# Four convolution layers on one core: norm rows of the first two channels by TensorE, and another order of loads and late stores between layers 0 and 1 and between 2 and 3

## The chip, the cores and the metric

One core of a Trainium2 chip. The metric is the device time of one execution in microseconds (us), lower is better; the kernel before and the kernel after are each run several times and medians are compared. A core has five engines, each with its own instruction stream that it works through in order: TensorE (PE, with its weight loads as PEld), VectorE (DVE), ScalarE (ACT), GpSimd (POOL), and SyncE (SP), which in this kernel does no arithmetic and issues all the DMA transfers. An engine whose next instruction has to wait holds up everything queued behind it.

## What is computed

The input x is 32 images of 96 channels of 56 by 56, float32. Four residual layers follow one another, each on a group norm without weights (32 groups of 3 channels):

```python
x = x + L0(gn(x))   # 1x1 expand to 576, 3x3 depthwise, squeeze-excite, 1x1 project, + its input
x = x + L1(gn(x))   # 5x5 depthwise plus a 3-level Haar wavelet of 5x5 depthwise filters
x = x + L2(gn(x))   # the expand/depthwise/project block with 4-bit weights and activations
x = x + L3(gn(x))   # 9x9 depthwise, kernel made from a 2x2 matrix per channel
```

The norm needs, for each image and group, a mean and a variance over all its 56 x 56 x 3 values. So no part of an image can be normalized until all of that image is there.

## The kernel before: how it works

**Layers 0 and 2** go image by image with channels on partitions; the order of their steps on TensorE, VectorE and ScalarE is written by hand as a string per image (`L0_ORDER`, `L2_ORDER`, `MANUAL`). **Layers 1 and 3** go channel by channel with image rows on partitions and the 32 images along the free dimension; a filter is a banded matrix, so that a depthwise convolution is a chain of matmuls (L918 in layer 1, L1416 in layer 3). Layer 1 takes two channels at a time (48 pairs), layer 3 one (96). In both the order of SP's instructions is by hand too (`MANUAL_SP`): what is written first is issued first. GpSimd's order is left to a scheduler.

**Between the layers** the activations go through DRAM (`y0`, `y1`, `y2`), because the next layer needs them the other way round. Each of these tensors is in six parts of 16 channels (`GR`), so the load of a channel waits only for the stores of its own part. An image is stored by `store_images` (L215), except the last: image 31 stays in SBUF (`kept`) and is stored in tiles by `store_tile` (L189), one tile being 16 channels by 14 rows, 49 KB: 4 tiles by 6 parts, 24 stores. The tiles of part 0 must be in DRAM before channel 0 can be loaded; the stores of the other parts may follow later. `LastStores` holds what is still to be issued, in the order part by part, and `left.issue(n)` issues the next n.

- Before, in layer 0 the step `add` (L556), which makes the last image's output, stores tiles 0 and 2 of part 0 itself, and the first call `left.issue(2)` in layer 1 stores tiles 1 and 3. After that 3 stores are issued per pair.
- In layer 2 `add` (L1296) stores tiles 0, 1 and 2, and `left.issue(1)` in layer 3 stores tile 3. After that 2 stores are issued per channel until none is left, the first four while the second and third channels ahead are fetched and the last in the loop of channel 7.

**The norm of layers 1 and 3.** `Norm` works out one row per channel: 32 scales, 32 biases (one per image) and one convolution bias, 65 numbers, with the 96 channels on partitions (`row`). The last image's column comes at the end: two group sums by TensorE (L123, L134), a power by GpSimd (L136), a product on VectorE (L149). In layers 1 and 3 rows of one channel are on partitions, so every partition needs the same 65 numbers. That is done through DRAM: `store` (L152) writes all rows to `norm`, and `load_norm` (L772, layer 1, one channel) or `load_norms` (L1393, layer 3, 8 channels at a time) reads them back with a broadcast over 128 partitions. Then VectorE makes x = X * scale + bias (L855, L856; in layer 3 L1408, L1409), and TensorE filters it.

**What else is at the start of a layer.** The banded matrices are loaded raw from DRAM (L755 to L757, and L827 for layer 1's second level, L829 for its third) and put in order by ScalarE (`arranged`, copies at L739 and L765, whose result is T). Layer 1 has three sets of tiles (`T3`, `T2`, `c2`) that GpSimd clears at L810; loads into T3 and copies into T2 wait for that. Four constant matrices, low1, up1, low2 and up2, are loaded at L793; `rounded` (L799) rounds the first two on VectorE. `images` loads one channel: X (L727) and two small halo loads (L730).

**SP's order around the change, before.** Into layer 1: tiles 0 and 2; low1, up1, low2, up2; for channels 0 and 1 the raw matrices with T3; tiles 1 and 3; norm store; X0, X1; norm rows 0 and 1; then per pair X, norm row, matrices for each channel and 3 stores. Into layer 3: tiles 0 to 2; raw matrices of channels 0 and 1; tile 3; X0; norm store; X1; norm rows of channels 0 to 7; X2, its matrices, 2 stores; X3, its matrices, 2 stores; then in the loop over channels norm rows (every eighth), X, matrices, 2 stores, and the output of the channel four behind (L1447).

All of SP's transfers share one queue. Their ends are counted on 8 semaphores in turn, so a transfer is not issued before the one eight ahead of it has landed.

Of the kernel before, what the change touches and what calls it, by code (L numbers as in the profile page):

```python
# [35 lines left out]
GR = 16  # L36
# [116 lines left out]


# [37 lines left out]
class LastStores:  # L192


    def __init__(self, nc, y, xt, first):
        self.left = [(lambda i=i, g=g: store_tile(nc, y, xt, i, g)) for g in range(C // GR)
                     for i in range(NP) if g or i in first]
# [32 lines left out]
def layer0(ctx, tc, S, x, w, y0, tables, aside, keep):  # L230
# [320 lines left out]
    def add(im, i):  # L551
        for n, to, of in ((i, slice(C), slice(C)), (LAST, slice(i * GC, (i + 1) * GC), slice(C, 128))):
            for t in range(2):
                at = (2 * t * 2 + n) * 2 * 2 * RT
                v = im["xt"][to, at : at + 2 * 2 * RT, :]
                nc.vector.tensor_tensor(v, im["ps"][i][of, t, :NT].rearrange("c (r q) -> c r q", q=W4), v, ALU.add)  # L556
        im["added"].add(i)
        if im["b"] == B - 1:
            for a in range(2):
                if i in LASTS[a] and im["added"] >= LASTS[a]:  # L560
                    for t in range(2):
                        tile_stats(nc, stats, im["xt"], 2 * t + a)
                        if a == 0:
                            store_tile(nc, y0, im["xt"], 2 * t, 0)
# [10 lines left out]
    def finish(im):  # L575
        b = im["b"]
        if b == B - 1:
            later.append(LastStores(nc, y0, im["xt"], (1, 3)))
            return
        sums(im, "s4", AF.Square, mv_all[:, b, 0:1], -1.0)  # L580
        t = sm.tile([C, 1], F32, tag="t4", name="t4")
        nc.vector.tensor_reduce(t, im["s4"], AX.X, ALU.add)
        nc.vector.tensor_scalar(mv_all[:, b, 1:2], t, 1.0 / HW, None, ALU.mult)
        if b % 2:
            fetch(b + 3)
        if b < B - 4:
            for start in aside[b :: B - 4]:
                start()
        del ims[b]
# [187 lines left out]
def layer1(ctx, tc, w, y0, left, made, norm, t1, t2, t3, y1, behind):  # L777
# [18 lines left out]
    def rounded(name, shape):  # L796

        t = cp.tile(shape, F32R, tag=f"{name}r", name=f"{name}r")
        nc.vector.tensor_copy(t, constant(name, shape))  # L799
        return t  # L800
# [11 lines left out]
    def load(i):  # L812
# [11 lines left out]
        def matrices(c):  # L824
# [3 lines left out]
            st["raw2"].append(raw)  # L828
            nc.sync.dma_start(st["T3"][c % 2 * HH : (c % 2 + 1) * HH, c % 2], t3[c])  # L829

        if i == 0:
            for c in range(2):
                matrices(c)
            left.issue(2)
            made.store(norm)
            for part in (images, factors):
                for c in range(2):
                    part(c)
# [5 lines left out]
        left.issue(3)  # L844
# [100 lines left out]
    def begin(st):  # L945
        for j in range(2):
            matrices1(st, j)
        for j in range(2):
            matrices2(st, j)
        for j in range(2):  # L950
# [14 lines left out]
    with tc.manual_schedule(engines=MANUAL_SP):  # L965
# [3 lines left out]
        up2 = constant("up2", [2 * HH, 2, 128])  # L969
        for i in range(-3, PAIRS):  # L970
# [133 lines left out]
def layer2(ctx, tc, S, k2, y1, y2):  # L1104
# [187 lines left out]
    def add(im, i):  # L1292
# [5 lines left out]
        if im["b"] == B - 1:  # L1298
            if i < NP - 1:
                store_tile(nc, y2, im["xt"], i, 0)  # L1300
# [23 lines left out]
    return LastStores(nc, y2, k2.pairs[0][:C, :, 1, :], (NP - 1,)), norm  # L1324
# [51 lines left out]
def layer3(ctx, tc, w, y2, left, made, norm, td, out):  # L1376
# [42 lines left out]
    with tc.manual_schedule(engines=MANUAL_SP):  # L1419
        for c in range(2):  # L1420
            matrices(c)
        left.issue(1)
        images(0)
        made.store(norm)
        images(1)
        load_norms(0)
        for c in range(2, AHEAD):
            images(c)
            matrices(c)
            left.issue(2)  # L1430
        for c in range(-2, C):
            if 0 <= c < C - AHEAD:
# [3 lines left out]
                left.issue(2)  # L1436
            cur, far = sts.pop(c, None), sts.get(c + 2)
            if far:
                far["nr"] = norms[(c + 2) // NN * NN][:, (c + 2) % NN]
                far["T"] = arranged(nc, io, far["raw"])  # L1440
            for h in range(2):
# [91 lines left out]
def layouts(a):  # L1533
# [34 lines left out]
    def phase_taps(v):  # L1568
# [49 lines left out]
        "group": group.astype(np.float32),  # L1618
        **lowest_bands(),
# [25 lines left out]
```

## Time and profile before

| | us |
|---|---|
| time before, median of 3 | 5744.32 (5729.87, 5744.32, 5744.75) |
| the profiled execution | 5746.33 |
| its span in the trace | 5744.5 |
| layer 1's first filter matmul (L918) starts | 2685.97 |
| layer 1's last matmul starts | 3576.2 |
| layer 3's first filter matmul (L1416) starts | 5302.37 |
| layer 3's last filter matmul starts | 5739.5 |

TensorE's granted clock was 0.985 of full speed on the mean. The profile gives times in microseconds from the start of the span. A line of a timeline has the start, the length, the engine, the line of the kernel, the operation, what it writes and reads, and how many instructions were joined into it; in brackets, how long the engine had been idle before and what it had waited for. `SPq` is SP's queue: a row is the issue of a transfer, not the transfer, which ends some microseconds later. In a group's line the figures after the bar are busy time, mean nanoseconds of one, and the engine's idle time just before these instructions with what ended most of it. In a line of waits: who waited, for whom, microseconds in total, times, longest.

### The profile page before, as it was taken

To read this page: it belongs to the slowest core of one execution; us is meant where nothing else is said; L and a number is where in the kernel's file an instruction comes from. 1 tells how busy PE (TensorE), PEld (TensorE's weight loads), DVE (VectorE), ACT (ScalarE), POOL (GpSimd) and SP (SyncE) were. 2 spreads that over 40 slices of the span, in tenths; PEclk is the share of its full clock that TensorE was granted. 3 is DMA by queue.
4 is the path that set the end of the run, shared out by engine and by line. 5 is a ranking of instruction groups with operands and counts; after the bars stand their busy time and mean duration, and the time that the engine had idled before them with its cause. 6 is when DMAs were issued, how large, how long until landed. Compare 5 with 4: busy or idle time off the path is not lost.

```text
span 5744.5 us, 137240 instructions
## 1 busy us (share of the span) xinstructions
PE 5495.9 (96%) x59696; PEld 3060.6 (53%) x59696; DVE 4696.0 (82%) x5406; ACT 4173.3 (73%) x6020; POOL 239.8 (4%) x158
## 2 busy tenths in 40 slices
PE   5999999999999999997999999899999999998999
PEld 2333333333333333333566665777788877776444
DVE  6999999999999999996776665776777777775677
ACT  5888888888888888884566554776777777775455
POOL 5000000000000000000000000000000000000000
PEclk9999999999999999997999999999999999999999
DMA  3122333232222332215566666579579696744888
GB/s 99 17 56 60 63 57 59 56 58 55 44 53 54 61 60 54 51 18 66 148 148 147 148 147 113 24 52 48 39 52 50 48 54 40 54 32 55 226 252 246
DMA packets 1306411, 454.31 MB, mean 79 GB/s; under 512 B 1123841, under 2 KB 1301753, under 8 KB 1303889
## 3 DMA queue, kind: packets, MB, share of 16 engines
q1 hardware_dynamic: 1305809, 445.54, 50.2%
q8 instruction: 468, 7.67, 0.6%
q14 instruction: 134, 1.10, 0.1%
HBM read 284.44 MB, written 214.08 MB: 87 GB/s over the span
## 4 chain that ended last, share of the span: by engine, by line
PE 81%; DMA 6%; ACT 5%; DVE 3%; issue 2%; SPq 1%; POOL 1%; ACTq 0%; DVEq 0%; POOLq 0%
PE psd L482 17%; PE psd L1250 13%; PE psj L537 10%; PE ps L415 7%; PE ps L1231 7%; PE pc L918 7%; PE pse L438 6%; PE psj L1289 4%; DMA X<-y 3%; DMA raw<-tdiff 2%; ACT hi L1203 2%; PE pc L906 2%; PE pa L880 2%; PE pc L896 1%; ACT u L1221 1%
## 5 line engine op out<-in xcount | busy, mean ns | idle before, releaser
L456 DVE SCALAR_TENSOR_TENSOR h<-hpad,l_wdw,h 128x3136 f32<-128x3136 f32 x512 | 1782.1, 3481 | 9.1
L482 PE MATMUL psd<-plane,filt 128*32 128x392 f32 (+5 forms) x16384 | 1083.9, 485 | 0.0
L1250 PE MATMUL psd<-apad,diag 64*64 64x392 bf16 x20736 | 919.0, 330 | 73.4 <-issue 69.7
L1250 PEld LDWEIGHTS <-diag 64*64 64x64 bf16 x20736 | 690.2, 107 | 297.1 <-issue 119.6
L482 PEld LDWEIGHTS psd<-plane,filt 128*32 128x32 f32 (+1 forms) x16384 | 389.7, 108 | 675.1 <-issue 622.3
L1221 ACT ACTIVATE u<-ps,o,s 128x784 int16<-128x784 f32 x576 | 536.8, 1003 | 159.0 <-PE ps L1231 140.8
L739 ACT COPY T<-raw 32x112 f32<-32x112 f32 (+2 forms) x1440 | 462.7, 384 | 255.5 <-DMA raw<-tdiff 207.0
L1221 ACT ACTIVATE a<-psd,o,s 128x784 int16<-128x784 f32 x448 | 423.8, 998 | 282.0 <-PE psd L1250 282.0
L415 PE MATMUL ps<-xn,l_wboth 96*128 96x392 f32 (+1 forms) x1536 | 465.3, 505 | 23.7 <-ACT xn L397 22.9
L456 DVE SCALAR_TENSOR_TENSOR hc<-hhalf,l_wdw,hc 128x1568 f32<-128x1568 f32 x256 | 473.6, 1850 | 16.1 <-ACT hc L449 9.5
L1231 PE MATMUL ps<-hi,l_w1q 96*128 96x392 f32 x1280 | 461.4, 360 | 9.3 <-ACT hi L1203 9.1
L918 PE MATMUL pc<-x,T 128*112 128x416 f32 (+1 forms) x1152 | 447.9, 525 | 18.8 <-DVE x L856 18.8
L1416 PE MATMUL pc<-x,T 128*112 128x416 f32 (+1 forms) x1152 | 422.3, 528 | 26.7 <-DVE x L1409 16.6
L1231 PE MATMUL ps<-lo,l_w1q 96*128 96x392 f32 x1280 | 436.2, 341 | 0.0
L438 PE MATMUL pse<-xn,l_wboth 96*32 96x392 f32 x4096 | 391.5, 500 | 3.4 <-ACT hab L459 3.4
L415 PEld LDWEIGHTS ps<-xn,l_wboth 96*128 96x128 f32 (+1 forms) x1536 | 219.1, 173 | 248.7 <-issue 53.8
L1416 PEld LDWEIGHTS pc<-x,T 128*112 128x112 f32 x1152 | 204.7, 179 | 243.8 <-issue 200.5
L459 ACT ACTIVATE hab<-psd,o,s 128x784 f32<-128x784 f32 x256 | 283.3, 1111 | 59.0 <-PE psd L482 57.0
L425 ACT ACTIVATE hpad<-ps,o,s 128x784 f32<-128x784 f32 x256 | 278.6, 1105 | 49.1 <-PE ps L415 47.7
L537 PE MATMUL psj<-h,wg 128*32 128x392 f32 x3072 | 306.1, 513 | 0.1
L537 PE MATMUL psj<-hab,wg 128*32 128x392 f32 x3072 | 304.4, 510 | 0.0
L918 PEld LDWEIGHTS pc<-x,T 128*112 128x112 f32 x1152 | 192.0, 179 | 165.5 <-issue 165.5
(260 smaller groups left out, 7675.8 us busy)
## 6 DMA issues: line engine op xcount, KB each, us to landing
X<-y SPq DMA_DIRECT2D x192, 392.0 KB
y<-xt SPq DMA_DIRECT2D x108, 392.0 KB
y<-y SPq DMA_DIRECT2D x96, 392.0 KB
out_dram<-y SPq DMA_DIRECT2D x96, 392.0 KB
twav<-zwav SPq DMA_DIRECT2D x768, 36.8 KB
y<-kept SPq DMA_DIRECT2D x72, 392.0 KB
xt<-y SPq DMA_DIRECT2D x60, 392.0 KB
xt<-in_x_dram SPq DMA_DIRECT2D x8, 2352.0 KB
```

The lines of the kernel that those rows point to most:

```text
L415: nc.tensor.matmul(ps[p, j, :NT], wexp[:, k * 128 : k * 128 + 128][:, m], im["xn"][:, j, rows, :].rearrange("c h w -> c (h w)"), start=Tru ...
L438: nc.tensor.matmul(ps[f * GC : (f + 1) * GC, half, :NT].rearrange("p (r w) -> p r w", w=W2), wexp[:, c : c + GC], im["xn"][:, f % 2, r0 : ...
L456: nc.vector.scalar_tensor_tensor(h2, taken(im, k, t), wdw[:, k, t : t + 1], h2, ALU.mult, ALU.add)
L459: nc.scalar.activation(view, ps, AF.Silu, bias=bi[1][:, c : c + 1], scale=sc[1][:, c : c + 1], accum_out=accum)
L482: nc.tensor.matmul(ps[at * GC : (at + 1) * GC, r, :NT].rearrange("p (r w) -> p r w", w=W2)[:, r0 - half * n : r1 - half * n, q0:q1], filt[ ...
L537: nc.tensor.matmul(ps[s * GC : (s + 1) * GC, t, :NT].rearrange("c (m r q) -> c r q m", m=2, q=W4), wg[p, k, c * GC : (c + 1) * GC], phases ...
L739: nc.scalar.copy(to.rearrange("x t (p s) -> x t p s", p=NPH), v[:, k])
L918: nc.tensor.matmul(ps[:PH, to], st["T"][j][:, h, k, :], st["x"][:, j, h, of], start=first and n == 0, stop=not first and n == NK - 1)
L1221: nc.scalar.activation(out, ps, AF.Identity, bias=o[:, c : c + 1], scale=s[:, c : c + 1])
L1231: nc.tensor.matmul(ps[:, j, :NT], w1[:, k * 128 : k * 128 + 128], im[part][:, r0 : r0 + RT, :].rearrange("c h w -> c (h w)"), start=(part ...
L1250: nc.tensor.matmul(ps[q, j, :NT].rearrange("p (r w) -> p r w", w=W), diag[p, k, t, :], v, start=(t == 0), stop=(t == 8))
L1416: nc.tensor.matmul(ps[:, :, to], st["T"][:, h, k, :], st["x"][:, h, :, of], start=(n == 0), stop=(n == NK - 1))
```

## The change

It concerns the two seams, 0 to 1 and 2 to 3.

1. `spread`: TensorE multiplies `row` by a constant `pick` (96 x 2 x 128; for channel c all of row c is ones, the rest zeros), which puts channel c's 65 numbers on all 128 partitions of PSUM; ScalarE copies both channels to SBUF (`nr0`). Channels 0 and 1 of layers 1 and 3 take their norm rows from there. The other channels load theirs from DRAM as before.
2. No stores inside `add`. All four tiles of part 0 go out in the first `left.issue(NP)`, in layer 0 in the order 0, 2, 1, 3, and behind the loads of constants (pick among them, 96 KB) and raw matrices.
3. The norm store goes behind X0 and X1, and in layer 1 the two T3 loads of the first pair behind that.
4. low1 and up1 are rounded by ScalarE.
5. The late stores: in layer 1 one per pair instead of three; in layer 3 one in the loop of every third channel (−2, 1, 4, ... 55) instead of two per channel.

The order of SP after, into layer 1: low1, up1, low2, up2, pick, raw matrices of channels 0 and 1, four stores, X0, X1, norm store, T3 twice. Into layer 3: pick, raw matrices, four stores, X0, X1, norm store, X2, norm rows of channels 0 to 7, matrices 2, X3, matrices 3, and the loop.

On TensorE the two small matmuls stand ahead of the first filter matmuls. On ScalarE the copy to `nr0` stands behind the copies that make T and T2 of the first pair in layer 1 (`matrices1`, `matrices2`), and behind those of channel 0 in layer 3. GpSimd's instructions are the same in number.

```diff
--- before.py
+++ after.py
@@ -151,6 +151,13 @@
     def store(self, dram):
         self.nc.sync.dma_start(dram, self.row)
 
+    def spread(self, to, pick, ps):
+
+        nc = self.nc
+        for c in range(2):
+            nc.tensor.matmul(ps[:, c, :], pick[:, c, :], self.row, start=True, stop=True)
+        nc.scalar.copy(to, ps)
+
 
 def run_steps(step, image, order, done=""):
 
@@ -192,9 +199,8 @@
 class LastStores:
 
 
-    def __init__(self, nc, y, xt, first):
-        self.left = [(lambda i=i, g=g: store_tile(nc, y, xt, i, g)) for g in range(C // GR)
-                     for i in range(NP) if g or i in first]
+    def __init__(self, nc, y, xt, order):
+        self.left = [(lambda i=i, g=g: store_tile(nc, y, xt, i, g)) for g in range(C // GR) for i in order]
 
     def issue(self, n):
         for store in self.left[:n]:
@@ -560,8 +566,6 @@
                 if i in LASTS[a] and im["added"] >= LASTS[a]:
                     for t in range(2):
                         tile_stats(nc, stats, im["xt"], 2 * t + a)
-                        if a == 0:
-                            store_tile(nc, y0, im["xt"], 2 * t, 0)
 
     def store(im):
         if im["b"] == B - 1:
@@ -575,7 +579,7 @@
     def finish(im):
         b = im["b"]
         if b == B - 1:
-            later.append(LastStores(nc, y0, im["xt"], (1, 3)))
+            later.append(LastStores(nc, y0, im["xt"], (0, 2, 1, 3)))
             return
         sums(im, "s4", AF.Square, mv_all[:, b, 0:1], -1.0)
         t = sm.tile([C, 1], F32, tag="t4", name="t4")
@@ -796,7 +800,7 @@
     def rounded(name, shape):
 
         t = cp.tile(shape, F32R, tag=f"{name}r", name=f"{name}r")
-        nc.vector.tensor_copy(t, constant(name, shape))
+        nc.scalar.copy(t, constant(name, shape))
         return t
 
     NF = 3
@@ -826,22 +830,26 @@
             raw = pool.tile([PH, NK * PH], F32, tag="raw2", name="raw2", bufs=4)
             nc.sync.dma_start(raw, t2[c])
             st["raw2"].append(raw)
+
+        def third(c):
             nc.sync.dma_start(st["T3"][c % 2 * HH : (c % 2 + 1) * HH, c % 2], t3[c])
 
         if i == 0:
             for c in range(2):
                 matrices(c)
-            left.issue(2)
+            left.issue(NP)
+            for c in range(2):
+                images(c)
             made.store(norm)
-            for part in (images, factors):
-                for c in range(2):
-                    part(c)
+            for c in range(2):
+                third(c)
             return st
         for c in (2 * i, 2 * i + 1):
             images(c)
             factors(c)
             matrices(c)
-        left.issue(3)
+            third(c)
+        left.issue(1)
         return st
 
     def normal(st, j, h):
@@ -947,6 +955,9 @@
             matrices1(st, j)
         for j in range(2):
             matrices2(st, j)
+        both = cp.tile([128, 2, 2 * B + 1], F32, tag="nr0", name="nr0")
+        made.spread(both, pick, psum.tile([128, 2, 2 * B + 1], F32, tag="w", name="pr0"))
+        st["nr"] = [both[:, j, :] for j in range(2)]
         for j in range(2):
             for h in range(2):
                 normal(st, j, h)
@@ -967,6 +978,7 @@
         up1 = rounded("up1", [128, 2, 2, 128])
         low2 = constant("low2", [PH, 2, 2 * HH])
         up2 = constant("up2", [2 * HH, 2, 128])
+        pick = constant("pick", [C, 2, 128])
         for i in range(-3, PAIRS):
             nxt, far = i + 1, i + 2
             if i + 3 < PAIRS:
@@ -1296,8 +1308,6 @@
             nc.vector.scalar_tensor_tensor(
                 v, im["ps"][i][:C, j, :NT].rearrange("c (r q) -> c r q", q=W4), s3, v, ALU.mult, ALU.add)
         if im["b"] == B - 1:
-            if i < NP - 1:
-                store_tile(nc, y2, im["xt"], i, 0)
             tile_stats(nc, parts, im["xt"], i)
 
     def store(im):
@@ -1321,7 +1331,7 @@
     }
     with tc.manual_schedule(engines=MANUAL):
         run_steps(step, image, L2_ORDER)
-    return LastStores(nc, y2, k2.pairs[0][:C, :, 1, :], (NP - 1,)), norm
+    return LastStores(nc, y2, k2.pairs[0][:C, :, 1, :], range(NP)), norm
 
 
 def diffusion_kernels(tc, cp, w, behind):
@@ -1417,27 +1427,33 @@
         nc.vector.tensor_tensor(st["y"][:, h], ps, st["X"][:PH, h], ALU.add)
 
     with tc.manual_schedule(engines=MANUAL_SP):
+        pick = cp.tile([C, 2, 128], F32, tag="pick", name="pick")
+        nc.sync.dma_start(pick, w["pick"])
         for c in range(2):
             matrices(c)
-        left.issue(1)
-        images(0)
+        left.issue(NP)
+        for c in range(2):
+            images(c)
         made.store(norm)
-        images(1)
+        images(2)
         load_norms(0)
-        for c in range(2, AHEAD):
-            images(c)
-            matrices(c)
-            left.issue(2)
+        matrices(2)
+        images(3)
+        matrices(3)
+        both = cp.tile([128, 2, 2 * B + 1], F32, tag="nr0", name="nr0")
         for c in range(-2, C):
             if 0 <= c < C - AHEAD:
                 load_norms(c + AHEAD)
                 images(c + AHEAD)
                 matrices(c + AHEAD)
-                left.issue(2)
+            if c % 3 == 1:
+                left.issue(1)
             cur, far = sts.pop(c, None), sts.get(c + 2)
             if far:
-                far["nr"] = norms[(c + 2) // NN * NN][:, (c + 2) % NN]
+                far["nr"] = norms[(c + 2) // NN * NN][:, (c + 2) % NN] if c >= 0 else both[:, c + 2]
                 far["T"] = arranged(nc, io, far["raw"])
+                if c == -2:
+                    made.spread(both, pick, psum.tile([128, 2, 2 * B + 1], F32, tag="c", name="pr0"))
             for h in range(2):
                 if far:
                     normal(far, h)
@@ -1616,6 +1632,7 @@
         "eye2": np.tile(np.eye(64, dtype=np.float32), (2, 1)),
         "eye4": np.tile(np.eye(32, dtype=np.float32), (4, 1)),
         "group": group.astype(np.float32),
+        "pick": np.repeat(np.eye(C, 2, dtype=np.float32)[:, :, None], 128, axis=2),
         **lowest_bands(),
         "grid": np.broadcast_to(grid, (C,) + grid.shape),
     }
```

## The prediction

> **What bounds the kernel now.** I read the page's groups first, for the engine that sets the length.
>
> ```profile
> PE 5495.9 (96%) x59696; PEld 3060.6 (53%) x59696; DVE 4696.0 (82%) x5406; ACT 4173.3 (73%) x6020; POOL 239.8 (4%) x158
> ...
> L918 PE MATMUL pc<-x,T 128*112 128x416 f32 (+1 forms) x1152 | 447.9, 525 | 18.8 <-DVE x L856 18.8
> L1416 PE MATMUL pc<-x,T 128*112 128x416 f32 (+1 forms) x1152 | 422.3, 528 | 26.7 <-DVE x L1409 16.6
> ```
>
> TensorE is busy for 5495.9 of 5744.5 us, but the change takes no matmul off it (it adds four rows). Only TensorE's idle time can be gained: 18.8 us ahead of the first filter matmul of layer 1 and 26.7 us at L1416, so I read the two places where the layers meet. First the timeline from the last image of layer 0 to the first filter of layer 1.
>
> ```profile
> 2654.96 0.92 SPq L189 DMA_DIRECT2D y<-kept  x2
> ...
> 2667.95 1.00 POOL L810 MEMSET T<- 56x280 f32 x2
> 2668.03 0.19 DVE L149 SCALAR_TENSOR_TENSOR row<-xt,row 96x32 f32<-96x32 f32 x1 [0.66 <-POOL row L136]
> 2668.14 5.36 DVE L799 CAST low1r<-low 128x512 fp32r<-128x512 f32 x1
> 2668.30 0.31 SPq L829 DMA_DIRECT2D T<-twav  x1
> ...
> 2670.97 0.90 SPq L189 DMA_DIRECT2D y<-kept  x2
> ...
> 2671.97 0.81 SPq L152 DMA_DIRECT2D norm<-row  x1
> ...
> 2675.54 0.30 SPq L727 DMA_DIRECT2D X<-y  x1
> ...
> 2679.11 0.92 SPq L772 DMA_DIRECT2D nr<-norm  x2
> ...
> 2684.25 0.92 DVE L855 TENSOR_TENSOR x<-X,nr 128x448 f32<-128x448 f32 x1 [10.43 <-DMA X<-y]
> ...
> 2685.97 4.58 PE L918 MATMUL pc<-x,T 128*112 128x448 f32 x6 [18.79 <-DVE x L856]
> ```
>
> The path: the stores of group 0 go out at 2670.97 (from the transfers' end events the last lands at 2675.47), only then X0 (2675.54), then the norm rows (2679.11, landing 2684.13), then the first x on VectorE at 2684.25, then TensorE at 2685.97. The norm row itself was ready at 2668.22 (2668.03 + 0.19), 16 us before x. What kept the stores back is in SP's waits:
>
> ```profile
> SPq L189 <- DVE kept L556: 38.2, 1, 38.2
> ...
> SPq L829 <- POOL T L810: 6.6, 1, 6.6
> ```
>
> SP stood 38.2 us for layer 0's last adds with the filter loads queued behind it, and 6.6 us more behind a T3 load that needs a memset of GpSimd; that memset ended at about 2668, and only then came the stores of tiles 1 and 3, whose data was ready at 2662.96. Now the end of layer 2:
>
> ```profile
> 5289.42 0.37 SPq L189 DMA_DIRECT2D y<-kept  x1
> ...
> 5291.77 0.19 DVE L149 SCALAR_TENSOR_TENSOR row<-room,row 96x32 f32<-96x32 f32 x1 [0.66 <-POOL row L136]
> 5292.18 0.32 SPq L727 DMA_DIRECT2D X<-y  x1
> ...
> 5296.85 0.34 SPq L1393 DMA_DIRECT2D nr<-norm  x1
> ...
> 5300.93 0.63 DVE L1408 TENSOR_TENSOR x<-X,nr 128x448 f32<-128x448 f32 x1 [8.98 <-DMA X<-y]
> ...
> 5302.37 2.50 PE L1416 MATMUL pc<-x,T 128*112 128x448 f32 x3 [11.45 <-DVE x L1409]
> ```
>
> The same chain: raw loads stand in front of the last store (ready 5287.69, issued 5289.42, landed 5292.16), then X0, which lands at 5295.54, its halos by 5296.62, then norm rows issued 5296.85 and landed 5300.76, x at 5300.93, TensorE at 5302.37. Last, the windows of layer 3 (columns: length, busy time and instructions of PE, PEld, DVE, ACT, POOL, then clock, DMA share, GB/s):
>
> ```profile
> 5332.00:5342.00 10.00, 6.76 (x19) 2.84 (x17) 3.48 (x6) 2.40 (x7) 0.00 (x0) 1.00 0.72 170
> ...
> 5332.00:5342.00 10.00, 6.76 (x19) 2.84 (x17) 3.48 (x6) 2.40 (x7) 0.00 (x0) 1.00 0.72 170
> ...
> 5402.00:5442.00 40.00, 40.00 (x113) 19.74 (x112) 32.14 (x56) 22.31 (x66) 0.00 (x0) 1.00 0.89 256
> ```
>
> While two stores go out per channel (to 5360), TensorE is busy 6.76 and 7.64 of 10 us; later 40.00 of 40. A settled channel takes 4.30 us, so 96 take 412.8; from 5302.4 to the last matmul's end at 5739.9 there are 437.5. The 24.7 lost are, by the starts of successive channels, 1.6 in the first channel (clock 0.82), 16.2 in channels 6 to 12, and about 7 in the other 82, mostly behind norm loads.
>
> **The change, part by part.** The profiled run took 5746.3 us, 1.8 above its span and 2.0 above the median 5744.32. Sums are made against 5746.3 and the answer is lowered by some 1 us, since three runs do not fix that offset.
>
> *Layers 0 to 1.* low, up, pick and the raw loads leave SP ahead of all stores. They need only buffers of layer 0 that are free by about 2634, so they land before 2640, and 12 loads come off SP between 2655 and 2671. The four stores stay in order of need: tiles 0 and 2 at 2655, tiles 1 and 3 at 2662.5 and 2663.0 instead of 2671.0 and 2671.4, 8.4 us sooner. Their flights are 2.88 and 4.08 us (rows before), so they land by 2667. X0 at 2667.0, flight 3.5 (2675.54 to 2679.08), halos 4.8: 2670.5 to 2671.8 at the worst. The norm store and two T3 loads come behind X0 and X1, and only channels 2 and 3 need that store.
>
> Norm rows of channels 0 and 1: row ready 2668.22 plus two matmuls of 65 columns. No such row is in the trace; the nearest is L134, a pair of 1-column float32 matmuls, 0.48 us for both, and at the other end a 392-column one of L438, 0.50 each. I take 1.0 for both, between 0.5 and 1.3. The ScalarE copy of 130 elements costs about 0.3 (T copies of 32x112: 0.32 each, 2.79 for nine). But ScalarE works in order, and the copy stands behind the six T copies of the second level (1.9 us), which wait for GpSimd's memsets of 2667.95 to 2668.95: 2668.95 + 1.9 + 0.3 = 2671.2. Without that queue it would be 2669.5. So x starts at about 2671.2, when X0's halos come too, against 2684.25: **13 us**.
>
> The two roundings move from VectorE to ScalarE, which is idle for 22.11 us before its first T copy; they are done by about 2641. On VectorE low1r took 5.36 us where up1r, of the same size, took 0.41: it ended when GpSimd's memsets did, at 2673.2. Left there it would now be on the path. One rule speaks against the 13 us. The Trainium skill ("SBUF — State Buffer", section "Who interferes with whom") says that VectorE and GpSimd share one pair of ports under an exclusive lock, and that who comes second waits the whole instruction. By row, low1r was shut out until 2673.2; were the new first x shut out in the same way, it would start at 2673.2 and the gain be 11. But the page limits this to copies and casts in two-port modes, and to two-input operations only against a GpSimd operation that reads SBUF. Memsets do not, and the trace agrees: L149, two inputs, ran 0.19 us at 2668.03 beside a memset. I keep 13, with 11 as the low end and 14 as the high.
>
> Does the head start last? Next loads: X2 lands near 2676 and its norm row (norm store, then load, 5.0 us each at most here) near 2678.2; channel 2 needs them near 2679.8. Cover 1.6 us; if it fails, TensorE waits for the difference only. In layer 1 a pair takes 18.03 us and TensorE never waits for SP, so one store per pair instead of three moves nothing there. All of layer 1 is TensorE's, and the chain of layer 2 hangs on its end: the 13 us go through. A reload of GpSimd's library, 8.78 us at 2791.9, moves to the start of layer 2, where GpSimd idles 16.31 us before its first pow: hidden, with 7.5 us of cover.
>
> *Layers 2 to 3.* pick and the six raw loads go first, from 5263 on; lanes behind them are held by the previous image's stores, landed by 5279.9, so nothing is late for 5281.7. The last store goes at 5287.7 instead of 5289.4 and lands at 5290.4 (flight 2.74); X0 follows at 5290.45, lands at 5293.8 (flight 3.36), its halos by about 5294.3. Norm rows by matmul and copy: 5291.96 + 1.0 + 0.3 = 5293.3, hidden behind X0 (ScalarE's T copies can be done before, raw being early). x at 5294.0 instead of 5300.93: **7 us** (5 if the halos take the 4.1 us of before's second one, 7.5 at best). Next late are channel 2's norm rows: store behind X1, load landing at 5301 to 5302, wanted at about 5304. Cover 2 us.
>
> *Stores of layer 3.* The loop's loads and the output are 7 DMAs, with two stores 9, with one 8. A DMA waits for the one eight before it, so at nine the output waits for its own loop's X: it was issued 5333.27, 5343.03 and 5348.65, X landing 5333.20, 5342.63 and 5348.59. A loop then lasts X's flight (5.0 to 6.5) plus some 0.8, 5.97 on the mean, (5.97 − 4.30)/2 = 0.84 us per store. With one per third channel, 20 stores lie in channels −2 to 55. At eight DMAs, X waits only for the previous X: at most 5.2 − 4.3 = 0.9 late per store, of which four channels of prefetch and the two loops between hide most; 0.25 each is my estimate, 5 us in all, between 0 and 20 × 0.84 = 17. Another rule: the Trainium skill ("DMA: Bandwidth & Descriptors", "Specifications") wants at least 512 bytes per transfer for line rate. A store is 896 packets of 56 bytes at about 9 ns on 16 engines, 0.5 us of all of them; at a DMA share of 0.89 a channel has 4.3 × 0.11 = 0.47 us free. One store a channel would just not fit; a third (0.17) does. So bandwidth adds nothing, and lanes decide. Kept: 24.7 − 1.6 − 8 − 5 = **10 us** (−2 to 15), the 8 being what norm loads cost in any case.
>
> Sum: 13 + 7 + 10 = 30; 5746.3 − 30 = 5716, and I say 5715.
>
> **The rivals.** *Stores cost the same wherever they stand* (0.84 each: lanes hold and no loop catches up): 16.2 was paid for 16, 16.8 is paid for 20, so only the starts gain, about 20 us less 1: 5726. For it: settled loops have little slack on SP (7 DMAs need 4.2 us). Against: a loop of eight DMAs no longer waits for its own X. *Stores free*: 13 + 7 + 15 = 35: 5710; the one-per-pair layer shows stores that cost nothing, but in a layer with four times the room. *Slower*: in layer 3 each store stops SP for its landing, 2.74 us or more, because a lane it took comes round in the next loop, and the queue never recovers: 20 × 2.74 = 55, less 16 saved, less 20 at the starts: 5763. It turns to a loss from (20 + 16) / 20 = 1.8 us per store; before's 0.84 with two stores in every loop speaks against it. *It doesn't do what it says*: the matmul rows wait behind ScalarE's queue and memsets, so that layer 1 gains 9 and not 13: 5719, inside the first case.
>
> **How the numbers follow.** As summed, 5709 to 5721: 0.62. Stores cost the same, 5721 to 5732: 0.22. Free, 5704 to 5709: 0.12. Slower, 5763: 0.04. The range 5704 to 5732 leaves out the slower case and the ends of others. A run can tell about 0.3%, 17 us, from no change, so 5727 is the bound: faster 0.85, same 0.11 (the upper half of the second case), slower 0.04.
>
> **What would show it.** Right: no norm load before the first x in either layer; X0 issued near 2667; the copy to nr0 ended near 2671; TensorE's first filter near 2673 and, counted from its layer's start, 7 us sooner in layer 3; settled pairs still at 18.03 us; TensorE at 10 of 10 us from channel 6 on but for losses near stores under 0.3 us each. Wrong: ScalarE waiting at the nr0 copy beyond 2673, X2's or channel 2's norm row as the new last wait, pairs longer than 18.03, GpSimd's reload ahead of the first pow of layer 2, or channels to 55 at 4.6 us instead of 4.3.

## The result and the profile after

The changed kernel takes 5741.73 us (median of 20 runs, 5731.4 to 5769.7) and the kernel before 5745.42 (20 runs, 5729.9 to 5761.4). The ratio is 0.9995 with an interval of 0.9984 to 1.0007: no difference that can be told. A gain of 30 us was forecast. The profiled execution of the changed kernel took 5762.69 us, 21 above its median, so its span is not compared with that of before; its stages are.

First the two groups of filter matmuls, as the page lists them.

```profile
L1426 PE MATMUL pc<-x,T 128*112 128x416 f32 (+1 forms) x1152 | 422.3, 525 | 33.0 <-DVE x L1419 18.5
L926 PE MATMUL pc<-x,T 128*112 128x416 f32 (+1 forms) x1152 | 446.0, 524 | 3.4 <-DVE x L864 3.4
```

Layer 1's filters now wait 3.4 us where they waited 18.8. Layer 3's wait 33.0 where they waited 26.7. The program is cut below at six points of TensorE's instructions: layer 0's last depthwise matmul, layer 1's first and last filter matmul, layer 2's first and last depthwise matmul, the first filter matmuls of channels 0 and 95 in layer 3. The lengths in us, from one profile each (e1 to e12 are the experiments below):

| kernel | 0 to 1 | layer 1 | 1 to 2 | layer 2 | 2 to 3 | layer 3 | span |
|---|---|---|---|---|---|---|---|
| before | 63.6 | 889.7 | 47.0 | 1654.6 | 25.1 | 433.2 | 5744.5 |
| change | 50.3 | 889.4 | 49.5 | 1671.6 | 21.7 | 445.0 | 5760.9 |
| e1 raw loads merged | 50.3 | 889.4 | 49.4 | 1644.9 | 18.3 | 421.9 | 5706.5 |
| e2 five ahead | 50.2 | 889.5 | 48.3 | 1663.0 | 19.8 | 443.4 | 5747.4 |
| e3 two per channel | 50.1 | 889.3 | 49.2 | 1651.9 | 18.5 | 442.7 | 5734.3 |
| e4 thin stores | 50.3 | 889.5 | 48.0 | 1654.1 | 20.5 | 427.4 | 5722.9 |
| e5 two tiles per store | 50.4 | 889.3 | 46.9 | 1657.4 | 22.6 | 439.6 | 5738.3 |
| e6 no late stores | 49.9 | 889.5 | 49.8 | 1651.1 | 23.0 | 417.5 | 5715.7 |
| e7 raw load split | 50.6 | 889.5 | 46.9 | 1641.9 | 23.4 | 507.6 | 5793.5 |
| e8 before, raw merged | 63.3 | 889.6 | 46.8 | 1656.1 | 28.3 | 422.9 | 5738.9 |
| e9 30 and 31 together | 49.9 | 889.4 | 49.5 | 1655.3 | 18.1 | 450.9 | 5746.7 |
| e10 e9 and merged | 50.4 | 889.4 | 46.8 | 1649.1 | 18.6 | 424.8 | 5711.8 |
| e11 rounding on VectorE | 53.3 | 890.7 | 49.2 | 1655.9 | 20.2 | 441.4 | 5744.6 |
| e12 only layer 1's part | 50.0 | 889.5 | 49.6 | 1652.5 | 25.4 | 432.4 | 5731.2 |

Layer 2, whose matmuls the change leaves alone, takes 1642 to 1672 us in these profiles. The twelve kernels with the new first seam have 1654.1 on the mean and the two without it 1655.4, so the 17 us by which the changed kernel's layer 2 is longer here than before's are put down to noise. Layer 3 has a spread too: e11 runs the changed kernel's layer 3 and took 441.4 us where the change took 445.0, so one profile tells layer 3 to some 3.6 us. The gain at the first seam is there, 13.3 us. It went in layer 3: 11.8 us longer, where 10 less were forecast.

The timeline of the changed kernel from layer 0 to 1:

```profile
2666.73 0.30 SPq L731 DMA_DIRECT2D X<-y  x1
...
2669.31 0.19 DVE L149 SCALAR_TENSOR_TENSOR row<-xt,row 96x32 f32<-96x32 f32 x1 [0.66 <-POOL row L136]
...
2669.60 1.09 PE L158 MATMUL pr<-row,pick 96*128 96x65 f32 x4 [1.14 <-issue]
...
2670.26 1.81 ACT L743 COPY T<-raw 112x112 f32<-112x112 f32 x6 [22.18 <-POOL T L814]
...
2671.92 0.84 POOL L814 MEMSET c<- 128x896 f32 x1
...
2672.10 0.27 ACT L159 COPY nr<-pr 128x130 f32<-128x130 f32 x1
2672.40 0.93 DVE L863 TENSOR_TENSOR x<-X,nr 128x448 f32<-128x448 f32 x1 [2.90 <-ACT nr L159]
...
2674.13 2.50 PE L926 MATMUL pc<-x,T 128*112 128x448 f32 x3 [3.45 <-DVE x L864]
```

X0 goes out at 2666.73 (2675.54 before), its last halo lands at 2671.55. The row is ready at 2669.50; TensorE spreads it in 1.09 us (1.0 forecast), ScalarE's copy follows six T copies that waited for the memset, and ends at 2672.37, 0.03 before x. No norm load stands ahead of x. x takes 0.93 us beside a memset as it took 0.92 without one (before, at 2684.25), so the port lock that the prediction weighed does not touch it.

From layer 2 to 3, the same view, and under it SP's waits in 5250 to 5302:

```profile
5280.42 6.39 SPq L1431 DMA_DIRECT2D pick<-in_pick_dram  x1
...
5292.64 3.19 SPq L196 DMA_DIRECT2D y<-kept  x4
...
5300.54 0.27 ACT L159 COPY nr<-pr 128x130 f32<-128x130 f32 x1 [5.08 <-PE pr L158]
...
5301.07 0.30 SPq L731 DMA_DIRECT2D X<-y  x1
...
5306.36 4.10 PE L1426 MATMUL pc<-x,T 128*112 128x448 f32 x6 [5.86 <-DVE x L1419]
```

```profile
SPq L1431 <- ACT a2c L1233: 5.7, 1, 5.7
SPq L731 <- DMA y<-kept: 5.1, 1, 5.1
```

`pick` waits at the head of SP's queue for 5.7 us, until ScalarE's last a2c. The row tells only that wait; its likely reason is that `pick` lies in memory that layer 2 uses until then. The raw loads come after, from 5286.86 on. When they are issued, image 30's last store is still in flight: it is the transfer eight before the first store of part 0, it lands at 5292.58, and that store goes at 5292.64, though its tile was ready at 5289. Four stores then go close together and land up to 5300.95; X0 waits 5.1 us for them. The norm rows were there at 5300.81, no longer in the way.

Last, windows of layer 3, with the columns that they have in the prediction. First, of the kernel before, the one behind the window of 6.76 us; then three of the changed kernel:

```profile
5342.00:5352.00 10.00, 7.64 (x14) 3.63 (x15) 6.44 (x12) 4.78 (x14) 0.00 (x0) 0.66 0.68 157
```

```profile
5332.00:5352.00 20.00, 20.00 (x57) 9.87 (x56) 14.88 (x26) 9.99 (x31) 0.00 (x0) 1.00 0.87 241
5372.00:5412.00 40.00, 35.64 (x97) 16.40 (x96) 28.93 (x51) 19.88 (x59) 0.00 (x0) 1.00 0.79 223
5412.00:5452.00 40.00, 34.41 (x95) 16.39 (x94) 27.29 (x48) 18.70 (x55) 0.00 (x0) 1.00 0.80 229
```

The stretch to 5362, which had been 6.76 and 7.64 of 10 before, is full: the first channels now lose nothing. But from channel 14 on TensorE has 35.64 and less of 40 us, where before had 40.00. The DMA share is lower there than in before's full stretch (0.79 against 0.89).

### The profile page after: what moved, and what is told of

It is laid out like the page before. It is cut to its first block, busy times and chain, and to the rows that moved or that the text cites. A ratio compares the mean times of both kernels' runs of the same rounds, so it can differ in the third digit from the quotient of the medians.

```text
span 5760.9 us, 137258 instructions
## 1 busy us (share of the span) xinstructions
PE 5502.6 (96%) x59704; PEld 3062.1 (53%) x59704; DVE 4692.3 (81%) x5404; ACT 4175.6 (72%) x6024; POOL 239.9 (4%) x158
## 4 chain that ended last, share of the span: by engine, by line
PE 81%; DMA 7%; ACT 5%; DVE 4%; issue 2%; POOL 1%; SPq 1%; ACTq 0%; DVEq 0%; POOLq 0%
PE psd L488 17%; PE psd L1262 13%; PE psj L543 10%; PE ps L421 7%; PE pc L926 7%; PE ps L1243 7%; PE pse L444 6%; DMA X<-y 4%; PE psj L1301 3%; PE pc L914 2%; ACT hi L1215 2%; PE pa L888 2%; PE pc L904 1%; ACT u L1233 1%; DMA raw<-tdiff 1%
## 5 line engine op out<-in xcount | busy, mean ns | idle before, releaser
L421 PE MATMUL ps<-xn,l_wboth 96*128 96x392 f32 (+1 forms) x1536 | 465.5, 505 | 23.9 <-ACT xn L403 23.0
L1426 PE MATMUL pc<-x,T 128*112 128x416 f32 (+1 forms) x1152 | 422.3, 525 | 33.0 <-DVE x L1419 18.5
L1426 PEld LDWEIGHTS pc<-x,T 128*112 128x112 f32 x1152 | 201.6, 177 | 253.2 <-issue 186.7
L431 ACT ACTIVATE hpad<-ps,o,s 128x784 f32<-128x784 f32 x256 | 278.3, 1103 | 49.5 <-PE ps L421 48.2
L448 ACT ACTIVATE plane<-pse,o,s 128x784 f32<-128x784 f32 x256 | 256.1, 1001 | 24.6 <-PE pse L444 19.9
```

What stands on the lines that cost most here:

```text
L421: nc.tensor.matmul(ps[p, j, :NT], wexp[:, k * 128 : k * 128 + 128][:, m], im["xn"][:, j, rows, :].rearrange("c h w -> c (h w)"), start=Tru ...
L1426: nc.tensor.matmul(ps[:, :, to], st["T"][:, h, k, :], st["x"][:, h, :, of], start=(n == 0), stop=(n == NK - 1))
```

## The experiments

They were made after the first result, to tell three causes apart. Theory A: the eight transfers in flight set the pace of layer 3 (a place among the eight is called a slot). Rival B: the packets of the stores hold up the others. Rival C: loads are issued too few channels ahead. A fourth cause, the time that SP's own instructions take, was not among them; the traces kept of these runs speak to it, and it is looked at behind e7. Ratios are to the kernel before. e4, e6 and e11 were run once each.

**e1: one transfer less per channel** (in layers 1 and 3, which share this helper).

```diff
-    nc.sync.dma_start(raw[LOW:PH, 1], t[c, LOW:PH])
-    nc.sync.dma_start(raw[PH:, 1], t[c, 128:])
+    nc.sync.dma_start(raw[LOW:, 1], t[c, LOW:].rearrange("(a p) x -> a p x", p=128 - PH)[::2])
```

> Change as made, but the two small raw loads of a channel (16 rows each) go in one transfer: 6 transfers per loop of layer 3 instead of 7, 7 with a store instead of 8; same bytes, same packets. Measured is the time from the first filter matmul of channel 0 to that of channel 95 in layer 3: 433.2 us before, 445.0 after. Theory A (eight transfers in flight set the pace: a store costs its slot, and a lead once lost is not won back): a loop with a store is then as light as a settled loop is now, 415 to 422 us, total 5718 or so. Rival B (the stores' 896 packets of 56 bytes hold up the other transfers): same packets, 442 to 447. Rival C (loads are issued too few channels ahead): 442 to 447.

Layer 3 takes 421.9 us, as A said. The whole takes 5709.8 us (median of 6 runs; 5718 expected), ratio 0.9947 (0.9929 to 0.9964), under both kernels. One window:

```profile
5352.00:5392.00 40.00, 38.10 (x106) 18.27 (x105) 30.02 (x52) 20.68 (x61) 0.00 (x0) 1.00 0.86 251
```

TensorE has 38.10 us of 40, and 38.82 in the next 40, with all stores in place, one per third channel. The same bytes and store packets moved, so neither B nor C alone can be it. SP's waits over 200 us of that stretch, first of the changed kernel (5370 to 5570), then of e1 (5345 to 5545); columns are us in total, times, longest:

```profile
SPq L734 <- DMA X<-y: 13.4, 17, 1.3
...
SPq L731 <- DMA X<-y: 6.5, 9, 1.3
```

```profile
SPq L734 <- DMA X<-y: 13.6, 31, 0.8
...
SPq L731 <- DMA X<-y: 0.8, 2, 0.6
```

The rows to read are those where X itself (L731) waits: 6.5 us for the X before it, longest 1.3, in the changed kernel, as A has it. In e1 0.8 us are left of that, and the waits of the halos (L734) are as long in total but in about twice as many pieces.

**e2: five channels ahead.**

```diff
-    AHEAD, NN = 4, 8
+    AHEAD, NN = 5, 8
         matrices(3)
+        images(4)
+        matrices(4)
```

> Change as made, but layer 3 loads five channels ahead instead of four. Rival C (too few ahead): the stalls go, 416 to 425 us from channel 0 to 95. Theory A (slots): the slots are the same, one more channel of lead is spent once, so 4 to 5 us less at most: 440 to 445. Rival B (packets): the same as A, 440 to 445. Start of layer 3 the same or 1 us later.

Layer 3 takes 443.4 us, within its spread: C falls. Ratio 0.9990 (0.9979 to 1.0000).

**e3: two stores per channel again.**

```diff
-            if c % 3 == 1:
-                left.issue(1)
+                left.issue(2)
```

(the new line stands inside the block that fetches channel c + 4)

> Change as made, but the late stores of layer 3 go as before, two per channel, in channels 0 to 9; seams and layer 1 as changed. Theory A: 0.84 to 1.0 us per store as before, for 20 stores, 17 to 20 us, less the lead of about 8 us that before's stores used too: 433 to 437 us from channel 0 to 95, and TensorE full after channel 15. Rival B: a store costs the same packets wherever it stands, 445. Total about 10 us under the change: 5730 to 5735.

442.7, not 433 to 437. The loss is in channels 5 to 13 again, so its place follows A, but its size does not: dense stores were not clearly cheaper than spread ones (25.2 us over e6's 417.5, 1.26 each, against 1.20 to 1.37). Two things can have made before cheaper. Four of its 20 stores of this kind stood in front of the loop. And its TensorE began layer 3 later against SP: channel 2's X had been issued 15.3 us before its first matmul, against 11.4 in e3 and 11.6 in the change. At 1.0 to 1.26 a store, four stores and 4 us of lead make 8 to 9 of the 9.5 us between the two kernels; this is an estimate, and they were not tried apart. Ratio 0.9995 (0.9985 to 1.0005); 5738.5 us in all, not 5730 to 5735.

**e4: thin stores**, and **e6: none.** Both leave out stores of the last image, so their output differs; layer 2 fills image 31's part of y2 (channels 16 to 95) once from image 1, so that nothing unwritten is read.

```diff
-    rows = slice(i * 2 * RT * NPH, (i + 1) * 2 * RT * NPH)
+    rows = slice(i * 2 * RT * NPH, i * 2 * RT * NPH + NPH if thin else (i + 1) * 2 * RT * NPH)
```

> Leaves out most of the last image's channels 16 to 95 between layers 2 and 3: each of the 20 late stores writes one fourteenth of its bytes (64 packets instead of 896), same number and places; the rest of that image's y2 is filled once, early in layer 2, with another image's values. Theory A (slots): a small transfer still takes its slot for some 2 us and more, so much of the loss stays: 432 to 445 us from channel 0 to 95. Rival B (packets): a fourteenth of the loss, 416 to 421.

```diff
-            if c % 3 == 1:
-                left.issue(1)
```

> Leaves out the 20 late stores of layer 3 (channels 16 to 95 of the last image, filled once early in layer 2 with another image's values). Gives the length of layer 3 without them: 416 to 418 us from channel 0 to 95 if what before lost in channels 6 to 12 (16.2 us) was all theirs. The stores of the change then cost 28 us, 1.4 each, and thin ones 10.

Without late stores layer 3 takes 417.5 us. A window of that run, at the place of the loss (the next 40 us are full too):

```profile
5372.00:5412.00 40.00, 40.00 (x113) 19.76 (x112) 31.41 (x55) 21.62 (x63) 0.00 (x0) 1.00 0.88 254
```

So the 20 stores of the change cost 445.0 − 417.5 = 27.5 us, 1.37 each; by e11's profile 23.9, 1.20 each. Thin ones cost 9.9, 0.50 each, between what A and B had said: the transfer itself counts, and so do its packets.

**e5: two tiles per store, ten stores.**

```diff
-    rows = slice(i * 2 * RT * NPH, (i + 1) * 2 * RT * NPH)
+    rows = slice(i * 2 * RT * NPH, (i + n) * 2 * RT * NPH)
...
-            if c % 3 == 1:
+            if c % 6 == 4:
```

> Change as made, but the late stores of layer 3 carry two tiles each (98 KB, 1792 packets) and go one per sixth channel, 10 instead of 20: same bytes and packets, half the slots. From channel 0 to 95 in layer 3 (before 433.2, change 445.0, thin stores 427.4). Theory A (slots): half of the change's store cost, 428 to 435 us. Rival B (packets): unchanged, 442 to 448.

439.6, between both again: 22.1 us for 10 stores. Let a store cost a as a transfer and b for each tile in it. The thin and the whole ones give a + b/14 = 0.50 and a + b = 1.37, so b = 0.94 and a = 0.43; for ten doubles that makes 10 x (0.43 + 1.88) = 23.1. With e11's 1.20 it makes b = 0.75, a = 0.45 and 19.5. The 22.1 measured lie between. Ratio 0.9992 (0.9979 to 1.0005). The trace of e5 shows where the tiles are paid:

```profile
5407.35 0.42 SPq L196 DMA_DIRECT2D y<-kept  x1
5407.87 2.49 SPq L1466 DMA_DIRECT2D out_dram<-y  x1
```

SP's row for the output behind a double store lasts 2.49 us here and 2.06 on the mean of nine; elsewhere its median is 0.37.

**e7: the large raw load in two halves.**

```diff
-    nc.sync.dma_start(raw[:, 0], t[c, :128])
+    for r in range(0, 128, part):
+        nc.sync.dma_start(raw[r : r + part, 0], t[c, r : r + part])
```

(part is 64 in layer 3)

> Change as made, but the large raw load of each channel in layer 3 is two transfers of 64 rows: 8 transfers per loop, 9 with a store; same bytes and packets. Theory A (slots): loops without stores get longer too, X waits for the X before it, at least 0.5 us on 90 loops: 480 to 520 us from channel 0 to 95, total 40 to 70 us over the change. Rival B (packets): 443 to 449.

507.6: one transfer more per channel, of no more bytes, costs 62.7 us, and one less (e1) saves 23.1. The number is A's, and B is refuted as the whole cause. Ratio 1.0109 (1.0081 to 1.0137). But the reason that A gives, X waiting for the X before it, is not what most loops of e7 show:

```profile
5388.82 0.33 SPq L731 DMA_DIRECT2D X<-y  x1
...
5393.42 0.46 SPq L731 DMA_DIRECT2D X<-y  x1
```

The eight transfers of this loop, the first X among them, follow each other with pauses of 0.1 us at most, and the loop lasts 4.60 us, more than TensorE's 4.30. SP's own rows fill it, and 56 of the 86 loops from channel 6 to 91 are of this kind. The table takes SP's time from the issue of X of channel 5 to that of channel 60 apart. "Rows" are SP's rows with the short pauses between them; "slot" is the time in which SP stood although its last row was over, because the transfer eight before the next had not landed (by the transfers' end events); the rest is some 3 us.

| kernel | us | rows | slot |
|---|---|---|---|
| e6 no late stores | 244.5 | 210.1 | 31.7 |
| e4 thin stores | 252.8 | 217.7 | 32.2 |
| e5 two tiles per store | 263.7 | 230.4 | 30.5 |
| change | 271.2 | 231.1 | 36.9 |
| e1 raw loads merged | 251.4 | 220.0 | 28.2 |
| e7 raw load split | 308.7 | 289.4 | 17.5 |

In e7 the waits for a slot shrink by 19 us against the change and SP's rows grow by 58. In e1 both shrink, by 9 and 11. Of the 26.7 us that 19 stores add to e6 in this stretch, 21.0 are rows and 5.2 are slots. So the count of transfers matters as A said, but mostly because each one takes SP's time. A store has a row of its own, 0.42 us, which is nearly all that a thin one costs, and its packets lengthen the rows behind it: output, X and first halo together take 1.51 us on the mean without a store (e6), 1.39 behind a thin one, 2.05 behind one of 896 packets and 3.38 behind one of 1792.

**e8: the kernel before with e1's edit.**

> The kernel before with the two small raw loads in one transfer, nothing else: 6 transfers per loop of layer 3, 8 with two stores. Theory A: the output no longer waits for its own loop's X, so the 16 us of channels 6 to 12 shrink to under 6, and the waits at norm loads go: 417 to 423 us from channel 0 to 95 against 433.2; total 10 to 16 us under before. Rival B: 430 to 434, total unchanged. Seams as before: 63.6 us and 25.1 us.

Layer 3 takes 422.9, as A had it, but not by the way that was expected: channels 7 to 12 still lose 11.2 us and not under 6, and what is gone are the waits behind the norm loads. From channel 17 on there is hardly any loss. The total is a miss: ratio 0.9994 (0.9985 to 1.0003) where 10 to 16 us were expected. In this profile 3 us were given back at the seam (28.3): image 30's stores landed 1.85 us after the last add of layer 2, where they had landed 7.8 before it. Where the rest of the 10 us went in the 20 runs is not known.

**e9: images 30 and 31 stored together**, **e10: that with e1's edit.**

```diff
-        store_images(nc, y2, im)
+        store_images(nc, y2, im, [0])
...
+    left.left[NP:] = [(lambda i=i, g=g: store_tile(nc, y2, k2.pairs[0][:C], i, g, slice(B - 2, B)))
+                      for g in range(1, C // GR) for i in range(NP)]
```

(`[0]` is the list of the parts of image 30 that are stored at once)

> Change as made, but of image 30 only part 0 (channels 0 to 15) is stored at once in layer 2; its other five parts go with image 31's late stores (packets of 112 bytes instead of 56, the same number, 98 KB per store). This takes five of the six transfers away that keep the queue busy for some 37 us before layer 2 ends. Theory (the gain at the seam 2 to 3 depends on when image 30's stores have landed): the stores of part 0 then go out as the adds end, TensorE starts layer 3 8 us after the last add (11.3 in the changed kernel's profile, 14.7 before), every time; last depthwise matmul to first filter 18 us. Rival (the seam is long because pick and the raw loads stand ahead of the stores): 21 us as now. Layer 3 from channel 0 to 95: 445 if the number of packets sets a store's cost, 455 to 465 if their bytes do.

> The last one with the two small raw loads in one transfer. Seam 2 to 3 18 us; layer 3 from channel 0 to 95 421 to 426 us (421.9 with the raw loads alone); layer 0 to 1 and layer 1 as changed. Total under both kernels, 5704 to 5714, ratio to before 0.993 to 0.995.

The seam is 18.1 and 18.6, TensorE starting 7.7 and 8.2 us after the last add: image 30's stores set it. Layer 3 of e9 has 450.9, between the 445 for packets and the 455 for bytes: the same number of packets with twice the bytes costs 33.4 us instead of 23.9 to 27.5, so a store's price goes by packets more than by bytes. The total of e9 is no gain, ratio 1.0002 (0.9993 to 1.0011). e10 has layer 3 as expected, 424.8, but its total is a miss: 5720.4 us, ratio 0.9971 (0.9960 to 0.9981), where 5704 to 5714 were expected. It is better than before and no better than e1; its stages, with layer 2 set aside, are 28 us under before's, and the runs show 17. The difference is not explained.

**e11: rounding left on VectorE.**

```diff
-        nc.scalar.copy(t, constant(name, shape))
+        nc.vector.tensor_copy(t, constant(name, shape))
```

> Change as made, but low1 and up1 are rounded by VectorE as before. If the cast is shut out by GpSimd's memsets (5.36 us in the profile before), it lasts until they end, and the first x comes 2.5 to 3 us later than in the changed kernel: 53 us from layer 0's last depthwise matmul to layer 1's first filter matmul, against 50.3. If not, both casts take 0.8 us together and end before x's other inputs are there: 50.3.

```profile
2670.83 5.36 DVE L803 CAST low1r<-low 128x512 fp32r<-128x512 f32 x1
...
2675.06 0.84 POOL L814 MEMSET c<- 128x896 f32 x1
...
2676.10 0.41 DVE L803 CAST up1r<-up 128x512 fp32r<-128x512 f32 x1
2676.43 0.90 DVE L863 TENSOR_TENSOR x<-X,nr 128x448 f32<-128x448 f32 x1
...
2678.14 2.50 PE L926 MATMUL pc<-x,T 128*112 128x448 f32 x3 [6.05 <-DVE x L864]
```

low1r again lasts 5.36 us, to 0.3 us after the last memset, up1r 0.41 behind it, and x comes at 2676.43. The first seam takes 53.3 us: this part of the change is worth 3 of the 13.

**e12: only the part at layers 0 to 1.**

> Only the part of the change at layers 0 to 1 (norm rows by TensorE, loads first, rounding on ScalarE, one late store per pair in layer 1); layers 2 to 3 as before. Segments: 50.3 us to layer 1's first filter matmul (63.6 before), layer 1 889.4 as before, seam 2 to 3 25 to 28, layer 3 433 from channel 0 to 95. If the head start goes through to the end, the total is 11 us under before (13 less 2 at the start of layer 2), ratio 0.998; if the layers behind eat it, 1.000.

The segments are as expected (50.0, 889.5, 25.4, 432.4), and their sum is 12 under before in the profile if layer 2 is set aside. The median, 5736.78 against 5739.68, has a ratio of 0.9993 (0.9981 to 1.0004): it holds both 11 us and none. The runs do not show the 11 us in the total, nor that they are lost.

## Why the prediction was wrong

The sum was 13 + 7 + 10 = 30 us. The profiles show 13.3, 3.4 and −11.8 for its three terms. The third one failed, and with it the forecast.

**The seam 0 to 1: right**, in size and steps: 13.3 us for 13. The copy behind the T copies was the last wait, as worked out.

**Its head start: nearly right.** Layer 1 is unchanged to 0.3 us with one store per pair, and GpSimd is in time: the first pow of layer 2 came 0.1 us after its input. (Of what the prediction calls a reload, before's trace shows 8.78 us in which GpSimd stood with nothing to wait for, and no view names its cause.) What was not foreseen is 1.7 us on the mean at the start of layer 2 (48.6 in the twelve kernels with the new seam, 46.9 in the two with the old one). In the changed kernel's profile the work up to layer 2's first expand matmul takes about as long as before (29.4 us against 28.8), but TensorE then ran at a clock of 0.50 in its first 10 us, against 0.77. The Trainium skill ("TensorE: Matmul & The Clock Gate", "What's actually happening") calls the window that decides this free-running; three of the twelve had 46.8 or 46.9 too, and these ran at 0.78 in the 10 us from their first expand matmul, where the two with the old seam have 0.77 and 0.78 and the slowest 0.50. So the time goes with the granted clock; what decides the clock was not tested.

**The seam 2 to 3: the mechanism right, two moments wrong.** "pick and the six raw loads go first, from 5263 on; ... nothing is late for 5281.7": pick had to wait for layer 2's last a2c, to 5286, and image 30's stores landed 2.5 us before the last add in this run and not 7.8. Over the runs with this seam unaltered, TensorE's start after the last add goes with that landing: 4.9 us before the add gives 8.1 (e3), 2.9 gives 10.1 (e4), 2.5 gives 11.3 (change), 1.7 gives 12.6 (e6). With the old order it had 14.7 and 15.0 when they landed 7.8 and 4.1 ahead (before and e12). So the 7 us are there when those stores are out of the way, as in e9, and 2 to 3 when not; 3.4 in the profile.

**The stores of layer 3: here the forecast failed.** The step was: "at most 5.2 − 4.3 = 0.9 late per store, of which four channels of prefetch and the two loops between hide most; 0.25 each ..., 5 us in all, between 0 and 20 × 0.84 = 17". The 20 stores cost 27.5 us (23.9 by e11's profile), beyond both ends, 1.2 to 1.37 each. No sum stood behind the 0.25, and three things around it were wrong.

- The two loops between hide nothing. TensorE's shortest channel is 4.30 us in every profile, so it catches nothing up; what could be won back is SP's lead, the time from the issue of a channel's X to its first matmul. It falls from 11.6 us at channel 2 to 7.5 at channel 13 and stays between 6.2 and 8.9 to the end, also behind the last store. In e1, with six transfers, it grows again behind the last store, from 7.7 at channel 60 to 10.9 at channel 95. Seven transfers leave SP nothing to catch up with: in e6 their rows take 3.8 us a loop and the waits for a slot 0.6, norm loads included. So the lead is spent once, on the first four stores (channels 1 to 13 lose nothing), and the other 16 cost 27.6 us over e6 up to channel 59, 1.7 each.
- The upper end was too low. "0.84 per store" divided before's loss as if 9 transfers were its only cause and two stores shared it; by e6's baseline the 16 stores inside before's loop cost 433.2 − 417.5 = 15.7, 1.0 each, and four more stood ahead of the loop for nothing. In the change all 20 are in the loop, and a start won at the seam is taken from the lead (see e3). By this account a stage that SP paces does not end sooner because TensorE begins it sooner; that was not tried by itself.
- "896 packets of 56 bytes at about 9 ns on 16 engines, 0.5 us ...; so bandwidth adds nothing". Counted in the trace between 5295 and 5298, where only stores are under way, some 700 such packets pass per us while the engines show themselves 0.4 busy. By that rate a store's packets take 896 / 700 = 1.3 us, an estimate (four in a row landed 1.6 to 2.0 us apart); b of 0.75 to 0.94 goes with that. The share of DMA in the profile understates these small packets, and the rule on 512 bytes, weighed against the row and put aside, pointed the right way.

So the rival called slower was right in its second half ("the queue never recovers"), at half its price: 1.37 per store for 2.74. It was given a chance of 0.04. Its first half, that a store stops SP until it lands, is not what happened: in the 200 us looked at under e1, SP waited for a store's landing twice, 0.7 us in all.

By stages, with the change's own profile but layer 2 set aside: −13.3 − 0.3 + 2.6 − 3.4 + 11.8 = −2.6 us; the ratio of the 20 runs gives −2.9 (from −9.2 to +4.0). So close an agreement is partly luck, since the seams and layer 3 differ by 2 to 5 us from profile to profile. The gain was made at the seams and paid back in layer 3.

Two small slips decide nothing: low1r ended at 2673.50 in the kernel before, 0.3 us after the last memset and not with it, and the norm loads, read as about 7 us, went into the sum as 8.

What stays open is why SP's rows lengthen behind a store of many packets, and what share of the 5.2 us of slots comes from longer flights of the transfers around it. No run changed SP's own time alone, for instance by issuing some transfers from another engine.

## What to carry to other kernels

Where one engine issues all transfers in order, count transfers per step of the loop, and the time that the engine needs to issue them, before counting bytes: here one per channel less was worth 23 us and one more cost 63. Work that is spread into a loop without slack on its issuing queue is not hidden by a lead: the lead pays for the first pieces, and every later one costs its full price. Price a transfer of small packets by how many pass per microsecond in the trace when nothing else runs, and by what the issuing engine's rows behind it lose, not by the busy share.

## What the runs showed of the hardware

- Packets of 56 bytes: recorded with 9 ns each, but some 700 per us through all 16 engines together, which is 23 ns per packet and engine.
- SP's row for the output of layer 3 lasted 0.37 us in the median, and 2.06 on the mean behind a store of 1792 packets (e5): the packets of a transfer can cost time on the engine that issues the next.
- A VectorE cast beside GpSimd's memsets lasted 5.36 us in two kernels and 0.41 after them; two-input operations beside the same memsets 0.93 and 0.19.
- Layer 2, with the same matmuls each time, took 1642 to 1672 us; the cause wasn't looked for further.
- The start of layer 2 took 46.8 to 49.8 us, with a granted clock of 0.78 in its first 10 us in the shortest and 0.50 in the longest.
